# Residual adds split and moved behind row-sum adds, a turned norm moved ahead of the last row-sum piece, and a third group's norm moved ahead of the first attention burst

## The chip, the cores and the metric

The kernel runs on one core of a Trainium2 chip. It takes fp32 inputs and gives an fp32 output. The metric is the device time of one execution in microseconds (us), the median of the runs shown. A profiled execution has a time of its own and, inside it, a span: from the first to the last instruction that the profiler saw.

The engines are named as in the profile: PE (matmuls), PEld (its weight loads, which overlap the matmuls), DVE (vector), ACT (activations and copies), POOL (general-purpose vector work), and SP, which here does nothing but issue DMAs. Every DMA of this kernel is issued by SP, one after another, in the order of the program. An SP instruction that has to wait holds up all DMAs behind it.

## The reference

There are 64 batches of 256 tokens with 512 features, and one 256 by 256 adjacency matrix for all of them. Cut to what matters:

```python
# layer 0
h = relu(layernorm(x))
H = h @ W                                  # 512 -> 256
e = leaky_relu(H @ a0 + (H @ a1).T)        # 256 x 256 a batch
p = softmax(e + NEG * (1 - adj))
x = x + concat([p @ H, H])
# layer 1
h = relu(layernorm(x))
q, k, v = h @ Wq.T + bq, h @ Wk.T + bk, h @ Wv.T + bv      # 8 heads of 64
s = where(adj == 0, -inf, q @ k.T / 8)
x = x + softmax(s) @ v @ Wo.T + bo
```

## The kernel before

**Tiles and groups.** The 64 batches are taken in 32 groups of two. A token tile is 128 tokens, so that a group has two batches of two tiles. The matrix products are done by a Strassen-like scheme of seven products of half size (`seven`, `operand_sums`), which needs a few sums and differences of the operands; POOL makes these sums for the projections (`sums`, `sums_xn`, `sums_r`).

**The pipeline over groups.** In the main loop (line 1108) the work of several groups is interleaved. Iteration g holds two steps, b = 0 and b = 1. Each step starts with the attention scores and exponentials of batch b of group g (`scores`, the letter S), and then deals out one piece at a time from several generators, in the order of a string of letters (`steps`, line 1106): `u` a product of the projections of group g + 1, `o` an output product of the batch before, `s` a piece of the first layer of group g + 2, `n` a piece of the first norm of group g + 3, `m` a masking of a pair of heads, `f` a piece of the softmax's row sums (`fold`), `r` half of the residual additions (`residual`), `v` the differences of v. A step of another form is written out for g = b = 0, and a list for the time before the loop (`order`, line 1086). The letters fix the order in which the program is written. A scheduler then places the instructions on the engines; calls through `not_sooner` are tied behind the instruction that the same helper issued last on that engine, so that for these the written order holds. PE's order is fixed by `matmul` and `transpose`.

**What ends a step.** At the start of the next step `weigh` is called. The row sums of the softmax have gone a long way by then: POOL adds the two key halves of p (`mask_pairs`, shown as `p<-p` on POOL), SP writes them to DRAM (`rows`) and reads them back with another layout (`parts`), POOL adds four parts in two additions (`add` in `fold`, line 926), DVE transposes and reduces them (`sum_up`) and takes the reciprocal (`compact`), and `weigh` spreads it with a DVE transpose into a tile `r`. PE meanwhile multiplies p with v (`pr`), and DVE scales that by r into `oT`. That frees the PSUM banks of `pr`. PE goes on with the next scores (`sc`), which take their banks out of a ring of five that they share with `pr`.

**A piece that shares the place.** In step b = 0 the last `s` before `weigh` brings the edge scores of the first layer: SP writes a small `line` to DRAM and reads it back to all partitions as `own`; ACT forms `e` from it with four activations; DVE applies the leaky ReLU to e in two instructions (`e<-e`), ACT the exponential. `own` and `r` lie in one buffer (tag `r`), so that r can be written only when ACT has read own. `e` and the `parts` of step 0 share a buffer too (tag `e`). On DVE the two `e<-e` stand ahead of `r`, and on ACT the exponentials of e stand ahead of those of the scores.

**The first norm.** `norm_T` in pieces: statistics and factors (DVE, then POOL's `pow`), normalised tiles `xn` (ACT), `turn` (two DVE transposes into `xt` and a DMA `passed` to DRAM), `fetch` (four DMAs `moved` back), `put` (ACT copies into `hT`). The `n` of step 0 nearest its end is `turn` of batch 0 of group g + 3.

**The residual.** `residual(g + 1)` adds the output bias `b_out` to x, two additions of 128x512 for each batch, on POOL (line 759).

Of the kernel before, what the change touches and what calls it, by code (L numbers as in the profile page):

```python
# [57 lines left out]
def bounded(  # L58
# [24 lines left out]
    vector, scalar, gpsimd, sync = (  # L83
        Remembers(e) for e in (nc.vector, nc.scalar, nc.gpsimd, nc.sync)
    )
# [29 lines left out]
    def after(instruction, name):  # L115

        tc.add_manual_dep(
            instruction.ins, name,
            mybir.DependencyInfo(mybir.DependencyClass.NoSync, mybir.DependencyReason.DATA),
            reason="the engine's order",  # L120
        )

    def not_sooner(engine, operation, *args, **kwargs):

        last = engine.last
        after(getattr(engine, operation)(*args, **kwargs), last)
# [627 lines left out]
    def residual(g):  # L754

        for b in range(GB):
            for t in range(NT):
                xt = xs[g, b][:, t, :]
                not_sooner(gpsimd, "tensor_add", xt, xt, b_out)
            yield  # L760
# [86 lines left out]
    def value_differences(g, b):  # L847

        v = qkv["v", g, b][0]
        not_sooner(gpsimd, "tensor_sub", v[:, 1, :], v[:, 1, :], v[:, 0, :])  # L850
# [30 lines left out]
    def mask_pairs(p, last_group):  # L881


        for i in range(HP):
            pair = p[:, 2 * i : 2 * i + 2]
            engine = gpsimd if last_group and i == 1 else vector
            not_sooner(
                engine, "tensor_mul", pair, pair, maskT[:, None, :, :].to_broadcast([P, 2, NT, N])
            )
            if last_group:  # L890
                yield
                continue
            last = gpsimd.last
            made = gpsimd.tensor_add(pair[:, :, 0, :], pair[:, :, 0, :], pair[:, :, 1, :])
            for other in [last, *sums_last]:
                after(made, other)
            yield
# [3 lines left out]
    def fold(g, b, p):  # L901

        if g == NG - 1:
            return
        compact = small.tile([P, NQ, N // S], F32, tag="compact", name=f"compact_{g}_{b}", bufs=2)
        row_sums[g, b] = compact
        pool, tag, bufs = (att, "e", 1) if b == 0 else (big, "hT0", 2)
        rows = []  # L910

        def put(quad):
            rows.append(dram.tile([P, QH, N], F32, tag="rows", name=f"rows_{g}_{b}_{quad}"))
            heads = slice(quad * QH, (quad + 1) * QH)
            not_sooner(sync, "dma_start", rows[quad], p[:, heads, 0, :])

        def fetch(quad):
            parts = pool.tile([P, P // S, N], F32, tag=tag, name=f"parts_{g}_{b}_{quad}", bufs=bufs)
            for j in range(QH):
                not_sooner(  # L920
                    sync, "dma_start", parts[j * S : (j + 1) * S],
                    rows[quad][:, j, :].rearrange("(i a) n -> a i n", a=S),
                )
            return parts

        def add(parts):
            not_sooner(gpsimd, "tensor_add", parts[:, :2], parts[:, :2], parts[:, 2:])
            gpsimd.tensor_add(parts[:, 0], parts[:, 0], parts[:, 1])

        def sum_up(quad, parts):  # L930
            not_sooner(vector, "transpose", parts[:, 1], parts[:, 0])
            vector.reduce_sum(
                compact[:, quad], parts[:, 1].rearrange("p (k a) -> p k a", a=S), axis=AX.X
            )

        put(0)
        parts = fetch(0)
        yield
        put(1)
        yield  # L940
        add(parts)
        yield
        sum_up(0, parts)
        parts = fetch(1)
        yield
        add(parts)
        yield
        sum_up(1, parts)
        vector.reciprocal(compact, compact)
        yield  # L950
# [47 lines left out]
    def outputs(g, b):  # L998
        xt, ops = xs[g, b], operands.pop(("o", g, b))

        def product(out, i, start):
            a, w = ops[i]
            for c in range(2):
                matmul(
                    out, a[:, c, :], w_sb["o"][:, c, w, :],
                    start=start and c == 0, stop=(c == 1), skip_group_check=True,
                )

        def add(t, half, out):
            to = xt[:, t, half * D // 2 : (half + 1) * D // 2]  # L1010
            vector.tensor_add(to, out, to)

        first = held_bank(2, f"py1_{g}_{b}")[:, : D // 2]
        product(first, 1, True)
        add(0, 0, first)
        yield
        second = mm(f"py2_{g}_{b}")[:, : D // 2]
        product(second, 2, True)
        add(0, 0, second)
        yield  # L1020
        product(first, 6, False)
        add(1, 0, first)
        yield
        second = mm(f"py7_{g}_{b}")[:, : D // 2]
        product(second, 7, True)
        add(1, 1, second)
        yield
        product(first, 5, False)
        add(1, 1, first)
        yield  # L1030
        product(second, 4, False)
        add(1, 0, second)
        if g == NG - 1:

            nc.sync.dma_start(og[g, b][:, 1], xt[:, 1])
            nc.sync.dma_start(og[g, b][:, 0, : D // 2], xt[:, 0, : D // 2])
        yield
        product(first, 3, False)
        add(0, 1, first)
        if g == NG - 1:  # L1040
            nc.sync.dma_start(og[g, b][:, 0, D // 2 :], xt[:, 0, D // 2 :])
        else:
            not_sooner(sync, "dma_start", og[g, b], xt)
        yield


    def run(part):
        for _ in part:
            pass
# [33 lines left out]
    next(norms)  # L1083
    next(verdict)
    next(verdict)
    order = "n - - - - - nss s s ss ss s s n n sn - s n".split()
    for i, parts in enumerate(order, 2):
        next(products)
        if i == 7:
# [13 lines left out]
    run(verdict)  # L1103


    steps = ("Smmnfuuuumonmnuofuusssosfsfssuvnofunofnosuo", "Srrsmmfusmusmfuososfuosfsuuonufounfouunsous")
    waiting, late, folds = None, iter(()), iter(())
    for g in range(NG):
        products = project(g + 1) if g + 1 < NG else iter(())
        pieces = first_layer(g + 2) if g + 2 < NG else iter(())  # L1110
        for b, parts in enumerate(steps):
            if g == b == 0:

                parts = "Smmnnuuuumnnfmnufuuvssssfsfssunfunfnsuu"
            elif g == NG - 1:
                parts = "Smmoomoomooo"
            if waiting is not None:
                weigh(*waiting)
                late = outputs(*waiting[:2])
            i, count = -1, sum(part not in "frv" for part in parts)  # L1120
            additions = residual(g + 1) if b == 1 and g + 1 < NG else iter(())
            for part in parts:
                i += part not in "frv"
                if part == "u":
                    next(products, None)
                elif part == "o":
                    next(late, None)
                elif part == "s":
                    next(pieces, None)
                elif part == "n":  # L1130
                    next(norms, None)
                elif part == "m":
                    next(masks)
                elif part == "f":
                    next(folds, None)
                    continue
                elif part == "r":
                    next(additions, None)
                    continue
                elif part == "v":  # L1140
                    if g < NG - 1:
                        value_differences(g, b)
                    continue
                else:
                    waiting = (g, b, scores(g, b))
                    masks = mask_pairs(waiting[2], g == NG - 1)
                    folds = fold(*waiting)
                if "v" not in parts and i == (count * 3 // 4, 6)[b] and g < NG - 1:
                    value_differences(g, b)
                if i == count // 2:  # L1150
                    if g == max(NG - 2, 0) and b == 1:
                        conclude()
                    if g + 3 < NG:
                        load(g + 3, b)
        run(products)
        run(pieces)
# [373 lines left out]
```

## Time and profile before

| what | value |
|---|---|
| time, median of 3 runs | 2442.91 us (2442.80 to 2443.98) |
| time of the profiled execution | 2442.23 us |
| its span | 2440.6 us |
| PE busy / DVE / POOL / ACT | 98% / 72% / 59% / 42% of the span |
| one group of two batches in the steady part | 74.2 us |
| mean granted TensorE clock | 0.997 |

The profiled execution is 0.68 us below the median. Time outside the span is 1.63 us. In a group's row the columns are line, engine, operation, what is written and read, shapes and count, then busy time with the mean of one, then the idle time of that engine just before it and what ended that idle time. A timeline row gives start, duration, engine, line, operation, tiles, shapes and count, and in brackets the idle time ahead. Nearly all helpers are recorded on line 35 or 137, so that tiles' names tell more than lines.

### The profile page before, as it was taken

How to read it: one execution, taken by the hardware profiler on the slowest of the kernel's cores; microseconds unless marked ns; L12 is line 12 of the kernel's file. 1: busy time of each engine (PE TensorE's matmuls, PEld its weight loads, DVE VectorE, ACT ScalarE, POOL GpSimd, SP SyncE). 2: the span in 40 equal slices, each digit the busy share in tenths (PEclk: the TensorE clock that was granted, in tenths of full speed). 3: DMA queues.
4: the chain of work that ended last, by engine and by line, in shares of the span. 5: the costliest groups of instructions: out<-in, count | busy, mean ns of one | idle time of the engine just before them, and what ended most of it. 6: DMA issues, size and time to landing. Idle time of an engine off the chain costs nothing.

```text
span 2440.6 us, 42947 instructions
## 1 busy us (share of the span) xinstructions
PE 2396.2 (98%) x15772; PEld 2014.3 (83%) x15772; DVE 1746.7 (72%) x3338; ACT 1023.1 (42%) x2017; POOL 1437.7 (59%) x1282
## 2 busy tenths in 40 slices
PE   8899999999999999999999999999999999999998
PEld 7778888888888888888888888888888888888886
DVE  7577767777767867667777678776677776777665
ACT  5443443434444444434444444444344344443431
POOL 3556666556565566565566655565655666555651
PEclk9999999999999999999999999999999999999999
DMA  6344454444445444544444544444554445444331
GB/s 194 100 124 136 134 155 149 147 151 133 140 149 164 143 139 134 156 147 155 149 131 138 154 153 144 142 134 152 151 163 145 129 137 155 149 146 150 105 109 50
DMA packets 272041, 343.76 MB, mean 141 GB/s; under 512 B 25424, under 2 KB 217168, under 8 KB 271824
## 3 DMA queue, kind: packets, MB, share of 16 engines
q1 hardware_dynamic: 271824, 340.95, 45.2%
q8 instruction: 126, 2.06, 0.4%
q14 instruction: 91, 0.75, 0.1%
HBM read 177.22 MB, written 163.64 MB: 140 GB/s over the span
## 4 chain that ended last, share of the span: by engine, by line
PE 92%; DVE 4%; DMA 2%; issue 1%; ACT 1%; SPq 1%; POOL 0%; ACTq 0%; DVEq 0%; POOLq 0%
PE py L137 16%; PE pv L137 15%; PE pq L137 15%; PE pk L137 15%; PE sc L137 10%; PE ph L137 8%; PE pr L137 7%; PE po L137 4%; DVE oT L35 1%; DVE e L35 1%; DVE xt L35 1%; SPq L35 1%; DMA own<-line 0%; DVE r L35 0%; DMA passed<-xt 0%
## 5 line engine op out<-in xcount | busy, mean ns | idle before, releaser
L35 POOL TENSOR_TENSOR p<-p 128x512 f32<-128x512 f32 x248 | 395.9, 1610 | 347.4 <-DVE p L35 347.4
L35 ACT ACTIVATE xn<-x,factor 128x512 f32<-128x512 f32 x256 | 194.4, 807 | 369.9 <-POOL factor L35 369.8
L35 DVE TENSOR_TENSOR p<-p,maskT 128x1024 f32<-128x1024 f32 x254 | 338.5, 1352 | 1.2 <-ACT p L35 1.2
L35 DVE TENSOR_TENSOR x<-py,x 128x256 f32<-128x256 f32 x448 | 186.3, 416 | 196.4 <-PE py L137 190.0
L35 POOL TENSOR_TENSOR parts<-parts 128x512 f32<-128x512 f32 x248 | 248.5, 1002 | 89.9 <-DMA parts<-rows 68.4
L35 ACT ACTIVATE p<-sc 128x512 f32<-128x512 f32 x512 | 261.2, 617 | 93.0 <-PE sc L137 74.8
L137 PE MATMUL sc<-q,k 64*128 64x256 f32 x2048 | 268.7, 391 | 20.1 <-DVE oT L35 19.7
L137 PEld LDWEIGHTS sc<-q,k 64*128 64x128 f32 x2048 | 212.4, 188 | 77.0 <-DVE oT L35 31.7
L35 POOL TENSOR_TENSOR factor<-factor,rexp 128x2 f32<-128x2 f32 x128 | 120.2, 939 | 255.4 <-DVE factor L35 255.2
L137 PE MATMUL py<-wo_sb,oT 128*128 128x256 f32 x1024 | 262.4, 379 | 0.6 <-DVE oT L35 0.6
L137 PE MATMUL pk<-hT,wk_sb 128*128 128x256 f32 x1024 | 244.7, 382 | 0.0
L137 PE MATMUL pq<-hT,wq_sb 128*128 128x256 f32 x1024 | 239.9, 382 | 0.0
L137 PE MATMUL pv<-wv_sb,hT 128*128 128x256 f32 x1024 | 237.0, 379 | 0.4 <-ACT kept_v L35 0.4
L137 PE MATMUL pr<-p,v 128*32 128x256 f32 x4096 | 234.2, 380 | 0.0
L137 PEld LDWEIGHTS pq<-hT,wq_sb 128*128 128x128 f32 x1024 | 191.9, 190 | 35.1 <-issue 9.9
L137 PEld LDWEIGHTS pk<-hT,wk_sb 128*128 128x128 f32 x1024 | 189.7, 190 | 33.8 <-issue 10.4
L137 PEld LDWEIGHTS py<-wo_sb,oT 128*128 128x128 f32 x1024 | 194.2, 190 | 28.2 <-DVE oT L35 1.1
L137 PEld LDWEIGHTS pv<-wv_sb,hT 128*128 128x128 f32 x1024 | 194.4, 190 | 27.2 <-ACT kept_v L35 0.8
L137 PEld LDWEIGHTS pr<-p,v 128*32 128x32 f32 x4096 | 126.8, 110 | 97.8 <-issue 19.9
L137 PE MATMUL py<-wo_sb,o_sums 128*128 128x256 f32 x768 | 197.6, 380 | 0.5 <-DVE x L35 0.5
L137 PE MATMUL pq<-sums,wq_sb 128*128 128x256 f32 x768 | 181.5, 379 | 0.9 <-POOL hT L35 0.9
L137 PE MATMUL pv<-wv_sb,sums 128*128 128x256 f32 x768 | 181.5, 379 | 0.0
(148 smaller groups left out, 4109.5 us busy)
## 6 DMA issues: line engine op xcount, KB each, us to landing
passed<-xt SPq DMA_DIRECT2D x124, 512.0 KB, 3.2
moved<-passed SPq DMA_DIRECT2D x496, 128.0 KB, 3.5
rows<-p SPq DMA_DIRECT2D x124, 512.0 KB, 3.4
parts<-rows SPq DMA_DIRECT2D x496, 128.0 KB, 3.0
x<-in_x_dram SPq DMA_DIRECT2D x64, 512.0 KB, 4.4
out_dram<-x SPq DMA_DIRECT2D x62, 512.0 KB, 4.0
own<-line SPq DMA_DIRECT2D x31, 256.0 KB, 3.2
wq_sb<-in_L_gnn_Wq_dram SPq DMA_DIRECT2D x2, 512.0 KB, 9.3
```

The lines of the kernel that those rows point to most:

```text
L35: instruction = getattr(self.engine, operation)(*args, **kwargs)
L137: in_order(nc.tensor.matmul(*args, **kwargs))
```

## The change

There are four edits.

1. In `add` of `fold` the second addition of parts is issued through `not_sooner`, so that it is tied behind the POOL instruction that was issued before it.
2. In `order`, the list for the time before the loop, the pieces of the third group's first norm stand earlier: six pieces of `norms` become eight, and the last six positions are dealt anew. The step for g = b = 0 has two `n` fewer and other places for the rest of them and for `f` and `v`.
3. In the string of step 0 the last `f o n` becomes `o n f`: the norm's piece (the turning) stands ahead of the last piece of the row sums.
4. In the string of step 1 the two `r` move from the front to places behind the two pieces that add parts.

```diff
@@ fold
         def add(parts):
             not_sooner(gpsimd, "tensor_add", parts[:, :2], parts[:, :2], parts[:, 2:])
-            gpsimd.tensor_add(parts[:, 0], parts[:, 0], parts[:, 1])
+            not_sooner(gpsimd, "tensor_add", parts[:, 0], parts[:, 0], parts[:, 1])
@@ before the loop
-    order = "n - - - - - nss s s ss ss s s n n sn - s n".split()
+    order = "n - - - - - nss s s ss ss s sn n n sn n sn -".split()
@@ the loop
-    steps = ("Smmnfuuuumonmnuofuusssosfsfssuvnofunofnosuo", "Srrsmmfusmusmfuososfuosfsuuonufounfouunsous")
+    steps = ("Smmnfuuuumonmnuofuusssosfsfssuvnofunonfosuo", "Ssmmfusmusmfuososfuosfrsuuonufrounfouunsous")
@@
             if g == b == 0:
-                parts = "Smmnnuuuumnnfmnufuuvssssfsfssunfunfnsuu"
+                parts = "Smmnfuuuumnmnufuussssfsfssuvnfunnfsuu"
```

In the program as it is built, PE's instructions keep their order. On the other engines:

- ACT, once, before the loop: the `xn` of the third group stand behind the third copy `kept_v` instead of ahead of it, and its second pair stands ahead of the second copy into `hT` and the last four exponentials of the first scores instead of behind them.
- DVE, in every step 0: the two transposes `xt<-xn` stand ahead of the last-but-one addition `x<-py` and of the transpose, sum and reciprocal of the second parts, instead of behind these. Before the loop, transposes move ahead of statistics and of the first masking. In every step 1 one statistics instruction changes places with two transposes.
- SP, in every step 0: `passed<-xt` stands ahead of `own<-line` instead of behind it.
- POOL, in every step 1: the four additions `x<-x,b_out` leave their place ahead of the first `p<-p`; two stand behind the additions of the first parts and ahead of the factors of the norm, two behind the additions of the second parts and ahead of `sums<-hT`. In the first group the subtraction `v<-v` moves behind two `x<-H,x`.
- PSUM banks, in step 1 of groups 1 to 28: the fourth tile of scores gets the bank of the first (freed by ACT's `p<-sc`), and the fifth that of the first `pr` (freed by DVE's `oT`). Before it was the other way round.

## The prediction

> **What bounds the kernel now.** I read the page's busy shares and chain first, then PE's waits between 160 and 2300 us, then the chain and timelines of one steady group (500 to 516 us), and last PE's timeline before the loop.
>
> ```profile
> PE 2396.2 (98%) x15772; PEld 2014.3 (83%) x15772; DVE 1746.7 (72%) x3338; ACT 1023.1 (42%) x2017; POOL 1437.7 (59%) x1282
> ...
> PE 92%; DVE 4%; DMA 2%; issue 1%; ACT 1%; SPq 1%; POOL 0%; ACTq 0%; DVEq 0%; POOLq 0%
> ```
>
> PE works 98% of the span. Only its gaps can be won; any edit can add one. PE's waits after 160 us:
>
> ```profile
> PE sc L137 <- DVE oT L35: 14.0, 29, 1.4
> ```
>
> There is one gap a group, 14.0 us in 29: 13.1 in groups 1 to 28 (mean 0.467; mostly 0.32 to 0.34) and 0.89 in group 29. The chain at 500 to 516 us (start, duration, work) shows it:
>
> ```profile
> 507.63 3.59 PE pr L137 x64
> 511.22 1.07 PE sc L137 x8
> 512.29 0.70 DVE oT L35
> 512.99 0.04 issue
> 513.03 2.85 PE sc L137 x22
> ```
>
> PE stops before the fourth score tile, wanted at 512.71, until `oT` frees its bank. Why `oT` is not earlier stands in the timelines of SP, ACT and DVE:
>
> ```profile
> 503.31 0.34 SPq L35 DMA_DIRECT2D own<-line  x1
> 509.43 0.34 SPq L35 DMA_DIRECT2D passed<-xt  x1
> ```
> ```profile
> 507.59 1.70 ACT L35 ACTIVATE e<-own,H 128x256 f32<-128x256 f32 x4
> 510.99 1.23 ACT L35 ACTIVATE e<-e 128x512 f32<-128x512 f32 x2 [1.70 <-DVE e L35]
> 512.31 1.09 ACT L35 ACTIVATE p<-sc 128x512 f32<-128x512 f32 x2
> ```
> ```profile
> 508.16 1.24 DVE L35 STREAM_TRANSPOSE xt<-xn 128x512 f32<-128x512 f32 x2
> 509.33 2.23 DVE L35 SCALAR_TENSOR_TENSOR e<-e 128x512 f32<-128x512 f32 x2
> 511.48 0.70 DVE L35 STREAM_TRANSPOSE r<-compact 128x512 f32<-128x512 f32 x1
> 512.28 1.29 DVE L35 TENSOR_TENSOR oT<-pr,r 128x512 f32<-128x512 f32 x2
> ```
>
> `own`, issued at 503.31, lands at 506.47; ACT has a microsecond in hand (`e` at 507.59). DVE's `e<-e`, `r` and `oT` then follow without slack. Two more rows price what the change touches: POOL's residual additions lie over the first `e<-e` (1.63 us; the second, alone, 0.68), and an `e<-e` pair without them takes 1.49:
>
> ```profile
> 505.42 4.98 POOL L35 TENSOR_TENSOR x<-x,b_out 128x512 f32<-128x512 f32 x4
> ```
> ```profile
> 69.29 1.49 DVE L35 SCALAR_TENSOR_TENSOR e<-e 128x512 f32<-128x512 f32 x2 [4.88 <-ACT e L35]
> ```
>
> Before the loop, PE's timeline has two long gaps, each followed by matmuls at half speed (`ph` 1.93 instead of 1.06, `sc` 5.14 instead of 2.85), and a 3.13 us gap that is not:
>
> ```profile
> 71.43 2.00 PE L137 MATMUL po<-H,e 128*128 128x257 f32 x8 [3.13 <-DVE e L35]
> ...
> 115.15 2.09 PE L137 MATMUL ph<-w_more,sums_xn 128*128 128x129 f32 x8 [3.29 <-POOL sums_xn L35]
> ...
> 140.55 5.14 PE L137 MATMUL sc<-q,k 64*128 64x256 f32 x22 [5.73 <-DVE oT L35]
> ```
>
> **The change, part by part.** The sum is made against the profiled execution, 2442.23 us; the median lies 0.68 above it.
>
> *The turning ahead of the last row sums (edit 3).* It removes and adds no instruction. DVE does the two `xt` (1.24 us) some 3.6 us earlier, at about 504.57 to 505.80, when `xn` (503.46 to 504.98) is ready; the `x<-py`, transpose, sum and reciprocal now behind it had 0.4 to 1.3 us of idle time on DVE ahead of them, waiting for PE, so they stay. The cost is on SP. `passed` (512 KB) is now ahead of `own` in SP's queue and waits for `xt`. It is issued at about 505.83, and `own`, 0.39 behind it, at 506.22 instead of 503.31: 2.91 us later. Behind `own` on SP nothing is urgent before `out_dram` (509.82).
>
> Call L the time from `own`'s issue to its landing. Alone it is 3.0 to 3.4, median 3.16 (31 times). Behind `passed` no row shows it. Bound below: 3.16, if it loses nothing. Bound above: transfers issued about 0.4 us behind a 512 KB one land later than the same kind alone: `out_dram` behind `passed` 4.03 for 2.80, `parts` behind `passed` 3.75 for 2.53, `x` behind `rows` 4.69 for 3.55. That adds at most 1.24, so 4.40. I take 4.0, nearer the upper end, because the two rows behind `passed` itself land at 3.75 and 4.03; `own` keeps the DMA engines only 0.43 busy while it runs, so that it may lose less than the 1.2 of the others.
>
> With 0.1 from landing to ACT, ACT starts `e` at T = 506.22 + L + 0.1 = 510.32 instead of 507.59. By the uncontended row (ACT `e` at 68.35, its exponentials done at 71.44) ACT is free for the scores' exponential 3.0 to 3.1 us later. PE's fourth score tile now waits for the bank that this exponential frees (0.6 us with its release). So PE resumes at T + 3.65 = 513.97 instead of wanting it at 512.71: a gap of L − 2.74 = 1.26 us. `oT` ends at T + 3.83, but only the fifth tile waits for it. Against the mean gap of 0.467, +0.79 a group; 28 groups: **+22.2** (L = 3.16: −1.3; L = 4.40: +33.4).
>
> The Trainium skill, "DMA: Bandwidth & Descriptors" (section "Anatomy of one DMA — SWDGE (gpsimd) path"), fits a DMA of that path as some 2.0 us plus its bytes at 436 GB/s. By that estimate `passed` and `own`, 768 KB in one stream, have landed 3.8 us after the first issue, at 509.6, with a gap of 0.66 us and +5.4 in all, so about 2447; but the fit gives `own` alone 2.6 us where the trace has 3.16, so the row decides.
>
> *Residual additions (edit 4).* Four additions, 4.98 us on POOL, go in two halves of 2.5. The first halves lie ahead of `factor`, where POOL idles at least 5.25 us, the second ahead of `sums<-hT`, at least 4.36: covered, cost 0. If that cover were gone, each half costs up to 2.5 us a group. The additions no longer slow the first `e<-e`: DVE's pair takes 1.4 instead of 2.3, counted above. Group 29 has no turning left, so only this relief acts: its gap of 0.89 falls towards the 0.3 of the common groups: **−0.6**.
>
> *Second addition of parts tied (edit 1).* In the steady loop its place on POOL is the same: 0, covered by its predecessor, which it follows directly. If something came between, one addition (under 1 us) on the row sums, which have 0.4 us at `r`.
>
> *Before the loop (edit 2).* The third group's `xn` go behind `kept_v`, so PE's 0.40 us wait at 87.64 for that copy goes: **−0.4**. What is late next is POOL's sums at about 98, with some 0.2 us to spare. The 3.29 gap stays: from the last `ph` over copy, `hT` and two POOL additions to the next `ph` the path is 5.2 us, none of it moved. At the 5.73 gap, `v<-v` goes behind two `x<-H,x` (128.2 to 129.4, wanted at 129.7), and `own` stays near 132.3 (132.40), lands up to 0.8 later behind `passed`, but its `e<-e` pair loses 0.9 of contention: 0, between −0.9 and +0.8.
>
> Half speed follows a gap of 3.29 us and not one of 3.13. It lasts 6.83 us and costs 3.4 at most: a gap that shifts may gain or lose 3 us. The Trainium skill, "TensorE: Matmul & The Clock Gate" ("What's actually happening"), has a free-running window of about 3.4 us that must be idle. By that rule 3.29 would not always halve the clock, and the phase decides; the trace agrees in so far that 3.13 did not and 3.29 did.
>
> Sum: 2442.23 + 22.2 − 0.6 − 0.4 = 2463.4, as a median **2464.1**.
>
> **Rivals.** Changes under 0.2% (4.9 us) can't be told from none.
>
> *B: `own` loses little behind `passed`.* For: alone it fills less than half of the DMA engines' time. Against: the three pairs above. For L up to 3.4 the gap is 0.42 to 0.66: −1.3 to +5.4, less 1.0, plus 0.68: 2440.6 to 2447.
>
> *C: faster.* DVE's relief decides. It needs `xt`, and with it `own`, some 0.2 us earlier than I place them or L at 2.9 to 3.05; then the gap falls to the floor of 0.26 that ACT's first score exponential sets (0.6 after a score tile that PE ends 0.34 earlier). 28 times 0.2 is −5.9, with −1.0: 2436, and 2433 if one slow clock is missed. From L = 3.05 on it no longer holds. Against: no `own` of 31 landed in under 3.0.
>
> *D: a second wait.* `e` ends 2 us later, and POOL's masks of it must be ready for `po` in the next step, where I count 1.0 us of slack (1.3 before). With that used up, or L over 4.4, another 0.5 us a group: above 2477.
>
> **How the numbers follow.** Forecast A (L 3.4 to 4.4, 2447 to 2475, at L = 4.0 2464.1): 0.61. B: 0.19. C: 0.07. D: 0.13. The range takes A and B: 2440 to 2476, leaving out C and D, 2 in 10. Faster is C, 0.07. Same is B, 0.19 (2438 to 2447.8). Slower is A and D, 0.74.
>
> **What would show it.** Right: `own` issued just behind `passed`, landing about 4.0; ACT waiting for DMA `own` in 28 groups; mean of `e<-e` from 1.2 to about 0.7 us; PE's gap at `sc` about 1.2 us, released by ACT's `p` instead of DVE's `oT`; POOL's waits at `factor` and `sums` shorter by 2.5 each; the gaps of 3.29 and about 5.7 still there. Wrong: L near 3.2 (B); an `sc` gap under 0.3 (C); a new PE wait at `po`, `py` or `ph` in the loop (D); or `xt` not moving forward because `xn` comes later, which would push `own` and the gap up by the same amount.

## The result and the profile after

The changed kernel takes 2504.61 us (median of 4, 2502.59 to 2508.65) against 2443.15 us (median of 4, 2442.80 to 2443.98) of the kernel before in the same job: a ratio of 1.0253, 95% interval 1.0235 to 1.0271. It is slower by some 61 us, nearly three times the 21 that were forecast. The profiled execution took 2504.86 us with a span of 2503.2 us, 62.6 more than before.

The page of the changed kernel, busy shares and the engines' shares of the chain:

```profile
PE 2416.1 (97%) x15772; PEld 2026.4 (81%) x15772; DVE 1703.9 (68%) x3338; ACT 1028.7 (41%) x2017; POOL 1427.8 (57%) x1282
...
PE 84%; DMA 5%; issue 4%; ACT 3%; DVE 3%; POOL 1%; SPq 0%; ACTq 0%; DVEq 0%
...
own<-line SPq DMA_DIRECT2D x31, 256.0 KB, 4.4
```

Two things stand here. DMA is on the chain now, and `own` lands 4.4 us after its issue (3.2 before). And PE is not only idle for longer: with the same 15772 matmuls it is *busy* 19.9 us longer. PE's waits after 160 us (engine, tile and line, what released it, total, times, longest):

```profile
PE sc L137 <- ACT p L35: 56.7, 28, 3.0
```

Before it was 14.0 us in 29, released by DVE's `oT`. The chain of one group, 519 to 529 us (start, duration, work), begins at the DMA:

```profile
516.44 4.45 DMA own<-line
...
521.14 1.72 ACT e L35 x4
522.86 0.02 issue
522.88 0.70 DVE e L35
...
524.14 0.59 ACT p L35
524.73 0.04 issue
524.78 2.85 PE sc L137 x22
```

SP's timeline of the same group shows why it begins late, DVE's that the two `e<-e` lost their old slowness:

```profile
515.99 0.34 SPq L35 DMA_DIRECT2D passed<-xt  x1
516.44 0.37 SPq L35 DMA_DIRECT2D own<-line  x1
518.23 0.39 SPq L35 DMA_DIRECT2D out_dram<-x  x1
```
```profile
522.08 1.49 DVE L35 SCALAR_TENSOR_TENSOR e<-e 128x512 f32<-128x512 f32 x2 [3.72 <-ACT e L35]
```

`passed` goes first, `own` follows after 0.45 us, `e` follows `own`, and the score exponential that frees PE's bank follows `e`. All of that was forecast. What was not forecast is in the next lines. PE's timeline at 443 to 452 us, one group earlier, and three windows of that stretch (window and length, then busy time and count of PE, PEld, DVE, ACT and POOL, the granted clock, DMA share, GB/s):

```profile
443.63 1.56 PE L137 MATMUL sc<-q,k 64*128 64x256 f32 x10
447.27 4.54 PE L137 MATMUL sc<-q,k 64*128 64x256 f32 x22 [2.08 <-ACT p L35]
```
```profile
441.00:444.00 3.00, 3.00 (x56) 1.71 (x50) 0.00 (x0) 0.36 (x1) 0.00 (x0) 1.00 0.72 225
444.00:447.40 3.40, 1.32 (x12) 0.85 (x10) 2.61 (x4) 3.23 (x8) 0.00 (x0) 1.00 0.43 125
447.40:450.80 3.40, 3.40 (x21) 2.82 (x22) 3.33 (x9) 2.58 (x5) 0.00 (x0) 0.62 0.10 39
```

The 22 score matmuls after the 2.08 us gap take 4.54 us, where those after the 1.96 us gap at 524.78 take 2.85. The granted clock falls to 0.62 in the window behind the gap. In the trace 12 of the 28 gaps in the loop are followed by such a stretch, 11 of about 3.4 us and one of about 6.

The time per group, over the same 22 groups of each profiled execution (from PE's records; the busy time of a tile is what it adds behind the matmul before it):

| us per group | before | changed |
|---|---|---|
| group | 74.33 | 76.63 |
| PE idle | 0.46 | 2.02 |
| `sc` busy | 8.19 | 8.93 |
| everything else of PE | 65.7 | 65.7 |

Over 28 groups the idle time is worth 43.7 us and the slower `sc` 20.6. Together that is 64.3, against 62.6 in the span; the rest is in the last groups and before the loop.

### The profile page after: what moved, and what is told of

It reads as the page before. It is cut to its first block, busy times and chain, and to the rows that moved or that the text cites. A ratio compares the mean times of both kernels' runs of the same rounds, so it can differ in the third digit from the quotient of the medians.

```text
span 2503.2 us, 42948 instructions
## 1 busy us (share of the span) xinstructions
PE 2416.1 (97%) x15772; PEld 2026.4 (81%) x15772; DVE 1703.9 (68%) x3338; ACT 1028.7 (41%) x2017; POOL 1427.8 (57%) x1282
## 4 chain that ended last, share of the span: by engine, by line
PE 84%; DMA 5%; issue 4%; ACT 3%; DVE 3%; POOL 1%; SPq 0%; ACTq 0%; DVEq 0%
PE pv L137 15%; PE pq L137 15%; PE py L137 14%; PE pk L137 13%; PE sc L137 9%; PE ph L137 8%; PE pr L137 5%; PE po L137 4%; DMA own<-line 4%; ACT e L35 2%; DVE e L35 1%; DVE xt L35 1%; ACT p L35 1%; DVE x L35 1%; SPq L35 0%
## 5 line engine op out<-in xcount | busy, mean ns | idle before, releaser
L35 POOL TENSOR_TENSOR p<-p 128x512 f32<-128x512 f32 x248 | 388.8, 1581 | 575.3 <-DVE p L35 571.6
L137 PE MATMUL sc<-q,k 64*128 64x256 f32 x2048 | 288.8, 413 | 62.6 <-ACT p L35 57.1
L137 PEld LDWEIGHTS sc<-q,k 64*128 64x128 f32 x2048 | 225.1, 199 | 124.2 <-ACT p L35 69.1
L35 POOL TENSOR_TENSOR factor<-factor,rexp 128x2 f32<-128x2 f32 x128 | 120.1, 938 | 172.0 <-DVE factor L35 171.8
```

The lines of the kernel that those rows point to most:

```text
L35: instruction = getattr(self.engine, operation)(*args, **kwargs)
L137: in_order(nc.tensor.matmul(*args, **kwargs))
```

## The experiments

The theory after the result: `own` behind `passed` on SP makes the whole loss, and the half clock follows from the longer gaps. The rivals: that POOL's moved additions, DVE's new order or the work before the loop take part in it.

**Edit 3 undone, and edit 3 alone.**

```diff
 e1: the changed kernel
-"Smmnfuuuumonmnuofuusssosfsfssuvnofunonfosuo"
+"Smmnfuuuumonmnuofuusssosfsfssuvnofunofnosuo"
 e2: the kernel before
-"Smmnfuuuumonmnuofuusssosfsfssuvnofunofnosuo"
+"Smmnfuuuumonmnuofuusssosfsfssuvnofunonfosuo"
```

> The changed kernel with the string of step 0 as before (edit 3 undone; edits 1, 2 and 4 stay), so that passed is issued behind own again. Theory (own behind passed makes the whole loss): own issued some 9.4 us ahead of the fourth score tile again, landing in 3.2 us; e<-e at 0.7 us each without the residual additions beside them; PE's gap at sc 0.26 to 0.35 a group, no half clock in the loop; 2434 to 2442 us. Rival (the residual additions on POOL, edit 4, take part in the loss): gaps of over 1 us a group or new waits of PE stay, 2460 us or more.

> The kernel before with edit 3 alone (the string of step 0). Theory: own issued 0.45 us behind passed, landing after about 4.4 us; PE's gap at sc about 2.0 us in 28 groups, released by ACT's p; half clock after some 12 of them; 2495 to 2510 us. Rival (the loss needs edit 4 as well): 2443 to 2470 us.

e1 took 2413.9 us, ratio 0.9887 [0.9867, 0.9906] to the kernel before; e2 2507.88 us, ratio 1.026 [1.024, 1.028]. Edit 3 alone makes the whole loss, and without it the rest of the change is a gain of over 1%. e2 is within its expectation: its gaps are 56.9 us in 28, and 12 of them are followed by half clock. The gain of e1 was a miss in the other direction: the best expectation was 2434 us, and e1 is 20 us below it. PE's waits after 160 us in e1 hold no `sc` at all any more:

```profile
PE py L137 <- DVE oT L35: 0.6, 1, 0.6
PE py L137 <- DVE x L35: 0.5, 2, 0.3
```

**SP's order alone.** DVE keeps the two `xt` early; only the DMA is tied behind `own`.

```diff
 e3: the changed kernel, in turn
-            sync.dma_start(passed[b], xt.rearrange("p j c t n -> p j (c t n)"))
+            operands = passed[b], xt.rearrange("p j c t n -> p j (c t n)")
+            if b == 0 and name in [f"0_{g}" for g in range(3, NG)]:
+                not_sooner(sync, "dma_start", *operands)
+            else:
+                sync.dma_start(*operands)
```

> The changed kernel with one more tie: passed of the third group's first half is tied behind the DMA issued before it, so that SP issues own first; DVE's order, with the two xt early, stays as in the changed kernel. Theory (the place on SP alone decides): own lands in 3.2 us as before, PE's gap at sc 0.26 to 0.35, no half clock in the loop, 2434 to 2442 us. Rival (the early xt delay DVE's row sums and r): gap stays over 1 us with a DVE release, 2470 us or more.

e3 took 2413.43 us, ratio 0.988 [0.9863, 0.9897]: the same as e1, again some 20 us below what was expected, and like e1 faster than both kernels of the case. So the early turning on DVE costs nothing; the place of one DMA in SP's queue costs some 90 us. `own` lands in 3.15 us again (median). In e3 as built the fourth score tile has the bank of `oT` again and the fifth that of the first score tile, as before. The exchange of the two banks in the changed kernel thus goes with the DMA's place, although no line on PSUM is touched, and e1, e2 and e3 alone can't tell the two apart: e1 and e3 have the banks of the kernel before, and e2, which changes nothing but the string, has the exchanged ones. e8, further down, can. It has a DMA ahead of `own` and the banks of the kernel before. PE's waits of e2 and of e8 after 160 us:

```profile
PE sc L137 <- ACT p L35: 56.9, 28, 3.0
```
```profile
PE sc L137 <- DVE oT L35: 48.7, 28, 2.2
```

So the exchange did not make the loss. It shortens the gap: with the exchanged banks (changed, e2, e6, e9) PE resumes 0.21 us before the first `oT` ends, with the others (before, e8) 0.06 us after it, a difference of 0.27 us.

**Edits 4 and 2 alone.** Edit 1 alone moves no instruction on any engine in the program as built, and was not run.

```diff
 e4: the kernel before
-"Srrsmmfusmusmfuososfuosfsuuonufounfouunsous"
+"Ssmmfusmusmfuososfuosfrsuuonufrounfouunsous"
 e5: the kernel before
-    order = "n - - - - - nss s s ss ss s s n n sn - s n".split()
+    order = "n - - - - - nss s s ss ss s sn n n sn n sn -".split()
...
-                parts = "Smmnnuuuumnnfmnufuuvssssfsfssunfunfnsuu"
+                parts = "Smmnfuuuumnmnufuussssfsfssuvnfunnfsuu"
```

> The kernel before with edit 4 alone (the two r of step 1 moved). Theory (the gain of e1 comes from DVE's e<-e, which the residual additions no longer slow, so that oT ends ahead of the fourth score tile): both e<-e at 0.69 us in all groups, no gap at sc, a group of 73.4 us for 74.3, 2413 to 2418 us. Rival (the gain comes from the work before the loop, edit 2): 2438 to 2443 us.

> The kernel before with edit 2 alone (the order before the loop and the first step's string). Theory: the gaps of 0.4 us at pv go and the one at pq grows to about 2.3 us; gaps in the loop as before, 0.3 to 0.5 us: within 4 us of before, 2438 to 2446 us. Rival (it carries the gain of e1): 2413 to 2420 us.

e4 took 2415.76 us, ratio 0.9886 [0.9871, 0.9901]; e5 2442.96 us, ratio 1.0005 [0.9995, 1.0014]. The gain of e1 is edit 4's; edit 2 does nothing that can be measured. In e5 the gap of 0.40 us at `pv` is gone, as expected, and the next one, before `pq`, has grown to 2.30 (0.92 before):

```profile
101.77 1.99 PE L137 MATMUL pq<-sums,wq_sb 128*128 128x256 f32 x8 [2.30 <-POOL sums L35]
```

Why edit 4 is worth 27 us, when all gaps of the loop together were 14.0, is to be seen in e4's group of `e<-e` on DVE (busy and mean of one, then idle time) and in PE's timeline:

```profile
L35 DVE SCALAR_TENSOR_TENSOR e<-e 128x512 f32<-128x512 f32 x64 | 40.6, 667 | 6.7 <-ACT e L35 6.4
```
```profile
508.99 3.92 PE L137 MATMUL sc<-q,k 64*128 64x256 f32 x32
512.84 1.99 PE L137 MATMUL pk<-hT,wk_sb 128*128 128x256 f32 x8
```

and in the same place of the kernel before:

```profile
511.15 1.56 PE L137 MATMUL sc<-q,k 64*128 64x256 f32 x10
513.03 2.85 PE L137 MATMUL sc<-q,k 64*128 64x256 f32 x22 [0.32 <-DVE oT L35]
515.81 1.99 PE L137 MATMUL pk<-hT,wk_sb 128*128 128x256 f32 x8
```

One `e<-e` takes 0.667 us for 1.205 before. From the first `sc` to `pk` it is 3.85 us in e4 and 4.66 us before: 0.81 us lost, of which the gap shows only 0.32. The score matmuls of two heads run side by side on 64 rows each: in the trace the two of a pair start 0.007 us apart. When one head's bank is not free, the other head's two matmuls run alone (before the gap at 513.03 they start at 512.12 and 512.33, 0.22 us apart), and PE counts as busy in that time. Over the steady groups `sc` is busy 8.19 us a group before and 7.70 in e4, the idle time 0.46 and 0. That is 0.96 a group (74.33 to 73.37), or 26.9 us over 28 groups.

**What makes `own` late.** In e6 `out_dram` is held until the next step's `rows` and `parts` are issued; in e8 and e9 `own_issue` is the instruction that issues `own`.

```diff
 e6: the changed kernel
-            not_sooner(sync, "dma_start", og[g, b], xt)
+            held_out.append((og[g, b], xt))
...
                     next(folds, None)
+                    while held_out:
+                        not_sooner(sync, "dma_start", *held_out.pop(0))
 e8: e6, in turn, first half of the third group
+                sync.dma_start(passed[b][:, : J // 2], flat[:, : J // 2])
+                after(sync.dma_start(passed[b][:, J // 2 :], flat[:, J // 2 :]), own_issue[0])
 e9: as e8
+                sync.dma_start(passed[b][: P // 8], flat[: P // 8])
+                after(sync.dma_start(passed[b][P // 8 :], flat[P // 8 :]), own_issue[0])
```

> The changed kernel with out_dram issued in the next step, behind the first rows and parts, instead of 1.79 us after own. Theory (own's 4.4 us are 3.95 behind passed, as in the first group where no out_dram follows, and 0.45 from out_dram): own lands after 3.9 to 4.0 us, gap about 1.6 us, 12 to 13 us less in gaps and no more half clocks than before: 2480 to 2493 us. Rival (own's landing is set by passed alone): own stays at 4.4 us, gap 2.0, 2500 to 2508 us.

> The kernel of e6 with passed of the third group's first half issued as two DMAs of 256 KB, one ahead of own and one behind it. Theory (what own loses is the time of the bytes ahead of it in the queue): own lands after 3.6 to 3.8 us, half way between 3.15 alone and 4.2 behind 512 KB; gap at sc about 1.2 to 1.4 us; half clock after few of these gaps, 0 to 3 of 28, since the shortest followed by it so far was 1.65 us; 2455 to 2468 us. Rival (a DMA ahead costs own a fixed time whatever its size): own 4.1 to 4.3 us, gap 1.6 to 1.8, 2480 us or more.

> As e8, but the DMA ahead of own carries 16 of the 128 partitions (64 KB), the one behind it the other 112 (448 KB). own is issued as late as in the changed kernel. Theory a (a DMA ahead costs own by its rows, 128 in the changed kernel and in e8, 16 here): own lands after 3.2 to 3.5 us, gap at sc 0.9 to 1.1 us, and no half clock after them, since none followed a gap under 1.6 us so far; 2450 to 2458 us. Theory b (any DMA 0.45 us ahead, or the one 0.42 us behind, costs own 0.85 us): own 3.9 to 4.2 us, gap 1.6 to 1.8 and half clock after some ten, 2490 us or more.

Times: e6 2487.05 us, ratio 1.0178 [1.016, 1.0196]; e8 2497.17 us, 1.0224 [1.0209, 1.024]; e9 2466.0 us, 1.0087 [1.007, 1.0103]. `own` stands in the pages of e6, e8 and e9 in this order:

```profile
own<-line SPq DMA_DIRECT2D x31, 256.0 KB, 4.1
```
```profile
own<-line SPq DMA_DIRECT2D x31, 256.0 KB, 4.0
```
```profile
own<-line SPq DMA_DIRECT2D x31, 256.0 KB, 3.7
```

The trace has 16 completions for each `own`. The table gives the first and the last of them, counted from its issue (medians):

| ahead of `own`, 0.4 us | behind it | first | last | mean gap | half clock after |
|---|---|---|---|---|---|
| nothing (before) | nothing near | 2.1 | 3.16 | 0.47 | 0 of 28 |
| 512 KB, 128 rows (changed) | `out_dram` 1.8 us later | 3.0 | 4.40 | 2.02 | 12 of 28 |
| 512 KB, 128 rows (e6) | nothing near | 3.0 | 4.10 | 1.65 | 8 of 28 |
| 256 KB, 128 rows (e8) | 256 KB 0.4 us later | 2.9 | 4.01 | 1.74 | 10 of 28 |
| 64 KB, 16 rows (e9) | 448 KB 0.4 us later | 2.25 | 3.65 | 1.15 | 4 of 28 |

e6 confirms that `out_dram`, issued after `own`, has a part in its lateness: 0.3 us of the 1.25, less than the 0.45 expected. e8 goes against the theory that the bytes ahead are what counts: with half of them, own's first completion comes almost as late, and its last at 4.01 instead of the 3.6 to 3.8 expected, just under the rival's 4.1. The gap and the time of e8 can't be set beside those of e6, though, as its banks cost it 0.27 us a gap; with the exchanged banks its gap would be about 1.47, by an estimate from these numbers. e9 lies between its two theories. With 16 rows ahead the first completion is nearly as early as alone, as the count of rows would have it; but the last comes 0.5 us late, with 448 KB behind. That a DMA ahead costs by its rows rather than its bytes fits all five lines, but it is not shown: the 16 rows of e9 are also the fewest bytes, 64 KB. That what comes behind delays the last completion fits e6 against the changed kernel, and e9. The effects were not separated further.

e9's time also came out 8 us above the upper end of theory a, because its mean gap was 1.15 us and four gaps of 1.53 to 1.89 us were followed by half clock.

## Why the prediction was right or wrong

**The direction and the chain of waits were right.** The forecast chain, `passed` ahead of `own`, `e` behind `own`, the scores' exponential behind `e`, PE's fourth tile behind that, is what the trace shows, with the releaser it named (ACT's `p` instead of DVE's `oT`) in all 28 groups. Undoing that one piece takes the loss away (e1, e3), and it alone makes it (e2). Two terms of the sum failed: L, and the half clock, which has no term at all for the loop.

**The term L was mis-sized.** It was taken as 4.0, with 4.40 as its end. Measured are a median of 4.40 over all 31 and, over the 28 groups, a mean of 4.55 with up to 5.5. The bound came from medians of other transfers, whose own longest were 5.4 and more, and each of the 28 groups pays its own landing. The step T = issue + L + 0.1 was short as well: from landing to ACT it is 0.21 us on average (0.25 in the group shown), and `own` is issued 6.37 us before the fourth tile is wanted instead of 6.49. From T to PE it is 3.63 us in every group, for 3.65 in the sum. So the gap is 4.55 + 0.21 + 3.63 − 6.37 = 2.02 us on average instead of 1.26: against the 0.467 before, 43.7 us over 28 groups instead of 22.2.

**The half clock in the loop was left out.** The prediction saw it before the loop, behind 3.29 us and not behind 3.13, and counted nothing for it behind the gaps of 1.26 us that it forecast in the loop. The runs show it behind gaps down to 1.53 us, and in the changed kernel, whose gaps are 2.02 on average, behind 12 of 28. It costs 20.6 us over 12 stretches, 1.7 us each. Without this term even the right L would have given some 2485 us.

**Edit 4 was priced by the visible gap.** "Mean gap of 0.467" was taken as all there was to win ("Only its gaps can be won"), and 0.26 as a floor under it. The stall really cost 0.96 us a group, since 0.49 of it runs as half-used score matmuls. Against e1 and e3 the floor fell too: it belonged to the banks of the changed kernel, and they come back when the DMA does. So rival C, had `own` stayed early and the banks with it, was worth 29 us and not 7. In the changed kernel none of that is seen, because the chain through `own` ends later than the one through DVE.

**Covered steps were covered.** POOL's additions found room where the prediction put them. POOL's wait at `sums` for ACT's `hT` fell from 147.7 to 70.2 us, the one at `factor` from 255.2 to 171.8: 77.5 and 83.4, or about 2.5 and 2.7 a group.

**Before the loop** −0.4 was forecast and nothing came (e5): the 0.2 us counted to spare ahead of `pq` was not there. In the kernel before PE already waits 0.92 us at that `pq` for POOL, and in e5 POOL's two additions ahead of it take 1.88 and 2.13 us for 1.45 and 1.28; why they do is not shown.

**Two rules that were weighed.** The estimate from "DMA: Bandwidth & Descriptors" (section "Anatomy of one DMA — SWDGE (gpsimd) path"), with `own` landed 3.8 us after the first issue, was too low here for two DMAs in a row: the measured 0.45 + 4.40 is 4.85. "TensorE: Matmul & The Clock Gate" ("What's actually happening") asks for an idle window of about 3.4 us before the clock halves. The length of 3.4 us is found again, as that of the slow stretches and of the grid on which they start. But the gaps of 1.53 to 3.01 us that were followed by half clock are shorter than the window that the page wants idle, and here the measurement decides.

## What to carry to other kernels

When a program is reordered, list for every queue what now stands ahead of the transfer on the path, its DMAs first: one tie on SP, the only edit between the changed kernel and e3, was worth 3.6% here. Look at the PSUM banks of the built program too, since they can change without an edit. Price a late transfer by the spread of its landings and not by their median, and look at what PE does behind a gap: 1.5 us of idle time can cost 1.7 us more in clock. And where two heads share the PE array, read the stall from the time between two fixed points of PE's order, not from the gap.

## What the runs showed of the hardware

- Half clock behind short gaps. In the changed kernel, e2, e6, e8 and e9, some of PE's gaps between 1.53 and 3.01 us were followed by a slow stretch, of 3.41 us in all cases but one; of the gaps under 1.5 us in the loops of any run none was. Neither length nor position alone decides: in the changed kernel a gap of 1.81 us was followed by it and one of 2.36 was not; in e2 one of 1.79 was and one of 2.50 was not.
- Length and position together tell more. In the trace's records of the granted clock the slow stretches of the loop start, within each of these runs, on one grid of 3.413 us, to within 0.01 us. Take the largest part of a gap that lies between two neighbouring points of this grid. Of the 140 gaps in the loops of these five runs, 65 have at most 1.52 us there, and none was followed by half clock; 16 have 1.97 us or more, and all were; of the 59 between, 30 were. The gap of 1.81 us lies whole between two points, that of 2.36 is cut into 0.69 and 1.67. What decides among the 59 is open. The 2.08 us gap shown above lies in the first of these two windows of the grid, and the granted clock is 0.50 in the whole of the second:

```profile
444.83:448.24 3.41, 1.33 (x11) 0.88 (x10) 3.17 (x6) 2.93 (x7) 0.00 (x0) 1.00 0.50 154
448.24:451.65 3.41, 3.41 (x16) 2.40 (x12) 3.38 (x7) 2.66 (x5) 0.00 (x0) 0.50 0.00 0
```

- A DMA of 16 rows and 64 KB ahead of `own` delayed its first completion by 0.1 us, one of 128 rows by 0.8 to 0.9, whether it moved 256 or 512 KB.
- A DMA that is issued 1.8 us later can still delay the one ahead: with `out_dram` out of the way `own` landed after 4.10 us instead of 4.40.
- Before the loop the clock differs from run to run for nearly the same gaps: the gap at `po` was followed by slow matmuls in e9 with 3.03 us and in e4 with 3.30, and not in e3 with 3.16.
